# Four graph layers on one core: layer 0's transpositions moved to the ends of its rounds, layer 2's to a spare bank, sigmoid's table loaded early

## The chip, the core and the metric

The kernel runs on one core of a Trainium2 chip. A core has five engines with an instruction order each: PE (TensorE, matrix products into PSUM), ACT (ScalarE), DVE (VectorE), POOL (GpSimd) and SP, which here only starts transfers. They run beside each other and meet at semaphores; each takes its own instructions strictly in order, so an instruction that waits holds up all behind it. The metric is the time of one execution in device microseconds, as the median of several runs.

## The reference

The inputs are `x` (4096 nodes by 64 features), a dense 4096 x 4096 matrix `adj` of zeros and ones with a density of about 0.001, and small weights. Four layers follow each other, each as `x = x + layer(relu(layernorm(x)), adj)`:

```python
# layer 0: attention between all nodes, masked by adj
h = lorentz_linear(x, W, b, scale)           # a linear map; column 0 becomes sigmoid(.)*exp(scale)+1.1,
q = lorentz_linear(h, Wq, bq, scale_q)       # the other 63 are scaled to fit it
k = lorentz_linear(h, Wk, bk, scale_k)
att = sigmoid((2 + 2 * (qm @ k.T)) / att_scale + att_bias)    # qm: q with column 0 negated
support = (adj * att) @ h
out = support / sqrt(clip(abs(support[:, :1]**2 - sum(support[:, 1:]**2)), 1e-8))
# layer 1: out = w @ (input @ weight) + bias; w halves with each further neighbour from the last, 100 of them
# layer 2: out = 1 - 0.1 * x - 0.01 * sum(x * (adj @ x), axis=1)
# layer 3: out = relu(concat([X, (adj @ X) / max(deg, 1)]) @ W.T)
```

## The kernel before

**Tiling.** The nodes are cut into 8 blocks of 512 (`ib`, the receiving nodes) and into 32 tiles of 128 (the sending nodes), taken in pairs (`g`). `adj` comes transposed, a pair of tiles by a block at a time. POOL loads each such piece into SBUF as an 8-bit mask (`load_masks`, L175; 128 pieces). SP loads all of `adj` once more in f32 in the background, and DVE checks that it holds zeros and ones only (`check`, L356; `ck` in layer 0, `ckw` later). If it does not, a general version of the model runs after this one (`model(True)`); it is in the program but not executed with these inputs.

**Prologue.** `first_rows_and_block` lists the rows' preparation (`before0`: norm, h, q and k) and the first block's work with a cost and an earliest time for each step. A planner (`Listing.plan` and `run`) tries many orders against these costs and writes the best one out; PE's idle stretches are filled with products that nobody reads (`fill`, L1039). The step `bias_rows` on POOL has a planned cost too. ACT needs tables for its functions: the `Exp` of L104 loads one set, and the first `Sigmoid` (L664) makes it load another.

**Layer 0.** After the prologue the order is written by hand. The loop over `todo` goes through rounds of `sizes` tiles: four in a steady block, with `first = [4, 4, 3, 3]` at the beginning. For each tile of a round `scores` (L920) makes 128 x 1024 products on PE into a PSUM tile `ps`, for which there are three places (two in `pp`, one in `spare`); `sigmoids` (L933) runs on ACT, and `masked` (L944) multiplies with the mask on DVE into an SBUF tile `att`. In a round of four, the first tile's sigmoid goes straight into `att`, so that ACT already releases its `ps`; the others' sigmoids stay in `ps` until DVE has multiplied them. After a round's scores PE makes the sums (`gather`, L951) of the round before. After each tile the loop calls `load_masks(1)`, at some tiles `check()`, and `on()`, which takes one step of the small jobs.

**Jobs.** A job is a generator: what it issues up to its next `yield` goes into the engines' orders at that point. `rows0` handles a finished block of layer 0. It lets two steps pass, turns the sums with four transpositions on PE (`turned`, L231, tile `pt`, in the bank `pr` of the pool `pm`), has ACT copy them out (`halves_added`, L237), adds halves on POOL (`sup`, L239), squares on ACT (L892), and reduces on DVE (the group `inn`, L895 to L898). A reciprocal root in twelve small POOL instructions follows (`rsqrt`, L260 to L263), and `x_sb` is updated on POOL (L900, L901). Then `norm` starts the next layer: `st` on DVE (L271, L272), `xc` on POOL (L275), a square on ACT (L278), the group `va` on DVE (L281, L291, L256), the root on POOL, and `xc` again on DVE (L297). `split` makes two f16 numbers of each feature in `s2a`: the first on POOL (L245), the second on DVE (L248) two steps later. `queries` prepares the next block's queries: it waits six steps, makes two transpositions (`pq`, L859, also in `pr`) and has ACT copy them into `qt` in four pieces (L869).

**Layers 1 to 3.** Layer 1 counts neighbours on PE (`many`, L1168; `cnt`, L1235 and L1245), turns the counts into weights on ACT and DVE (`w`) and sums (L1273). Layers 2 and 3 sum with masks as one operand (`product`, L1345); every fourth product takes a step of the jobs (`beat`). `rows2` evacuates a block's sums, turns them in bank 3 (`turned`, L231), and later uses the banks 3 and 4 again: `ph` (bank 4, L1410) for transpositions, and `pn` (banks 3 and 4, L1422) for the products with layer 3's weights, which ACT copies into `fa` and `v` (L1430, L1431). The bank `pr` of `pm` is used in layer 1 by `rows1` and has no user in layer 2.

Of the kernel before, what the change touches and what calls it, by code (L numbers as in the profile page):

```python
# [11 lines left out]
F32 = mybir.dt.float32  # L12
# [4 lines left out]
AF = mybir.ActivationFunctionType  # L17
# [7 lines left out]
P = 128  # L25
# [23 lines left out]
def kernel(  # L49
# [12 lines left out]
    nc = tc.nc  # L62

    cpool = ctx.enter_context(tc.tile_pool(name="const", bufs=1))
# [37 lines left out]
    part = cpool.tile([P, QUAD], BF16, name="part")  # L102
    exp_s = cpool.tile([P, 3], F32, name="exp_s")
    nc.scalar.activation(exp_s, scal[:, 0:3], AF.Exp)  # L104

    att_a = cpool.tile([P, 1], F32, name="att_a")
    att_c = cpool.tile([P, 1], F32, name="att_c")
# [26 lines left out]
    def model(general):  # L134
# [15 lines left out]
        def rows_in(gr):  # L150
# [10 lines left out]
        todo = [  # L161
            (ib, g) for ib in order0 for g in (first_cols if ib == order0[0] else range(NG))
        ]
# [21 lines left out]
        s2a = parts.tile([P, NT, 2, D], FP16, name="s2a" + sfx)  # L185
# [53 lines left out]
            nc.gpsimd.tensor_tensor(to, v[:, :, 0:D], v[:, :, D:P], ALU.add)  # L239
            yield  # L240

        def split(h, s2, rows):


            nc.gpsimd.tensor_scalar(s2[:, rows, 0, :], h, 1.0 / STEP, None, ALU.mult)  # L245
            yield
            yield
            nc.vector.scalar_tensor_tensor(  # L248
                s2[:, rows, 1, :], s2[:, rows, 0, :], -STEP, h, ALU.mult, ALU.add
            )  # L250
# [599 lines left out]

        stream0 = pool("stream0", 1, l0) if general else None
        spare, turn = [], [0]
        qts = {}

        def queries_turned(ib, pt):
# [16 lines left out]
            qts[ib] = qt  # L872

        def queries(ib):
            for _ in range(6):
                yield
            pt = pm.tile([P, CI, P], F32, tag="pr", name=f"pq_{ib}{sfx}")
            queries_turned(ib, pt)
            yield
            queries_laid(ib, pt)  # L880

        def rows0(ib, asb):
            tag = f"0_{ib}"
            rows = block(ib)
            yield
            yield
            pt = turned(asb, None, tag)
            yield
            sup = rows_tile("sup", tag)
            yield from halves_added(sup, asb, pt)  # L890
            sq = rows_tile("sq", tag)
            nc.scalar.activation(sq, sup, AF.Square)  # L892
            yield
            inn = small("inn", tag)
            nc.vector.tensor_reduce(inn, sq, AX.X, ALU.add)  # L895
            nc.vector.scalar_tensor_tensor(inn, sq[:, :, 0], -2.0, inn, ALU.mult, ALU.add)
            nc.vector.scalar_tensor_tensor(inn, inn, -1.0, inn, ALU.mult, ALU.max)
            nc.vector.tensor_scalar(inn, inn, 1e-8, None, ALU.max)  # L898
            rs = rsqrt(inn, tag)
            nc.gpsimd.tensor_tensor(sup, sup, bc(rs, CI), ALU.mult)  # L900
            nc.gpsimd.tensor_tensor(x_sb[:, rows, :], x_sb[:, rows, :], sup, ALU.add)  # L901
            yield
            yield
            yield
            yield
            h = yield from norm(rows, None, tag, False)
            yield from split(h, s2a, rows)
            ready.setdefault(1, set()).add(ib)

            nc.gpsimd.tensor_tensor(  # L910
                x_sb[:, rows, :], x_sb[:, rows, :], over_rows(bias1, CI), ALU.add
            )
# [43 lines left out]
        def first_rows_and_block():  # L956


            listing = Listing()
            add = listing.add  # L960
            bias = add("POOL", 3.8, lambda _: bias_rows(), at=6.5)
            for n in range(0 if general else len(todo) * EARLY // NIB * 5 // 8):
                add("POOL", 0.56, lambda _: load_masks(1), at=2.2 * max(n - 5, 0))
            made = [before0(listing, gr, bias) for gr in range(len(ROWS))]
            v = SimpleNamespace(att=[], pt={}, acc=None, at=0)
            asked = {}
            last = NIB - 1

            def turn_q(ib):
                def emit(part):  # L970
                    v.pt[ib] = turn_tile(part, f"pq_{ib}")
                    queries_turned(ib, v.pt[ib])
                return emit

            for ib in (last, last - 1):
                hw, fq, ktd = made[0]
                q = add(
                    "PE", 0.45, turn_q(ib), fq[max(fq)], *asked.values(), takes=TURN
                )
                asked[ib] = add(  # L980
                    "ACT", 1.5, lambda _, ib=ib: queries_laid(ib, v.pt[ib]), q, frees=q
                )

            def make_room(_):
                v.acc = pa0.tile([P, IB], F32, tag="pa", name=f"acc0_{last}{sfx}")

            room = add("PE", 0.0, make_room, asked[last], takes=("pa",))
            slots = tuple(f"att{n}" for n in range(ATTS))
            scored, spread = [], []
            for n, (ib, g) in enumerate(todo[: NG + 2]):  # L990
                gr = next(i for i, (r0, m) in enumerate(ROWS) if r0 <= g * CG < r0 + m)
                hw, fq, ktd = made[gr]
                u = (g * CG - ROWS[gr][0]) // HR
                tile = SimpleNamespace(ib=ib, g=g)
                begun = n >= NG

                def emit_scores(_, tile=tile):
                    tile.ps = scores(tile.ib, tile.g)

                def emit_sigmoids(_, tile=tile):  # L1000
                    tile.att = sigmoids(tile.ps, att_tile(tile.ib, tile.g))

                def emit_masked(_, tile=tile):
                    masked(tile.ib, tile.g, tile.att, tile.att)
                    if tile.ib != last:
                        v.att.append((tile.ib, tile.g, tile.att))

                def emit_gather(_, tile=tile):
                    gather(v.acc, fb, tile.g, tile.att, v.at)
                    v.at += 1  # L1010

                sc = add(
                    "PE", 0.88, emit_scores, ktd[u], asked[ib], *(scored if begun else ()),
                    takes=("pp0", "pp1"), form="scores",
                )
                sg = add(
                    "ACT", 1.2, emit_sigmoids, sc, *(spread if begun else ()), frees=sc,
                    takes=slots,
                )
                mu = add("DVE", 1.25, emit_masked, sg)  # L1020
                if begun:
                    continue
                scored.append(sc)
                spread.append(sg)
                add("PE", 0.88, emit_gather, mu, hw[u], room, frees=sg, form="gather")


            v.idle = pp.tile([P, CG, IB], F32, tag="pp", name="idle" + sfx)
            v.filling = 0

            def fill(part):
                if part.engine != "PE" or v.filling is None:
                    return
                if part.form == "scores":
                    v.filling = None
                    return
                for _ in range(int((part.idle - 0.1) / 0.215) if v.filling else 50):
                    v.filling += 1
                    nc.tensor.matmul(  # L1039
                        v.idle[:, v.filling % CG, :], ones,  # L1040
                        ones.unsqueeze(1).to_broadcast([P, IB // P, P]),
                        start=True, stop=True, skip_group_check=True,
                    )
                v.filling = max(v.filling, 1)

            listing.run(("pm", "pa", "ps", "pp0", "pp1", *slots), fill)
            return v.acc, v.att

        with tc.manual_schedule():
# [20 lines left out]
            k, done = NG + 2, NG  # L1070
            for size in sizes:
                now = []
                for ib, g in todo[k : k + size]:
                    ps = scores(ib, g)

                    if size == 4 and not now:
                        att = frm = sigmoids(ps, att_tile(ib, g))
                    else:
                        frm, att = sigmoids(ps), att_tile(ib, g)
                    masked(ib, g, frm, att)  # L1080
                    now.append((ib, g, att))
                    load_masks(1)
                    k += 1
                    if k > 2 * NG and k % 8 in (0, 2, 4, 5, 7):
                        check()
                    on()
                for ib, g, att in late:
                    at = done % NG
# [6 lines left out]
                        push(rows0(ib, evacuated(ib, acc, 0)), 10)  # L1095
                    done += 1
                late = now
            if len(checks) % 2:
                check()
            if general:  # L1100
# [284 lines left out]
        def rows2(ib, acc):  # L1385
            tag = f"2_{ib}"
# [2 lines left out]
            asb = evacuated(ib, acc, 2, sums_level, third=ib % 3 == 2)  # L1389
            yield  # L1390
            yield
            pt = turned(asb, 3, tag)
            yield
            prod = rows_tile("prod", tag, epi2)
            yield from halves_added(prod, asb, pt)
# [197 lines left out]
```

## Time and profile before

| | |
|---|---|
| median of the runs | 599.48 us (599.21 to 599.6, 3 runs) |
| the profiled execution's own time | 599.52 us |
| its span | 597.7 us |
| granted TensorE clock, mean | 0.997 |
| busy share of the span | PE 97%, DVE 81%, ACT 56%, POOL 40% |
| prologue | 0 to about 47 us |
| layer 0 | to about 299 us |
| layer 1 | to about 461 us |
| layer 2 | to about 528 us |
| layer 3 | to the end |

The span runs from the first to the last event of the profiled execution; its own time has 1.8 us around the span. A row such as `L944 DVE TENSOR_TENSOR att<-ps,mask` names the line of the kernel, the engine, the operation, and what it writes and reads. `PEld` is PE's weight load, which overlaps with the products. "Idle before" and the name behind it say how long the engine stood still ahead of an instruction, and what ended that. In the timeline, instructions of the same kind that follow each other are one row (`x4`), with the start of the first and the time until the end of the last; f32 products appear as two instructions each, so a tile of scores is x4.

### The profile page before, as it was taken

How to read it: one execution, taken by the hardware profiler on the slowest of the kernel's cores; microseconds unless marked ns; L12 is line 12 of the kernel's file. 1: busy time of each engine (PE TensorE's matmuls, PEld its weight loads, DVE VectorE, ACT ScalarE, POOL GpSimd, SP SyncE). 2: the span in 40 equal slices, each digit the busy share in tenths (PEclk: the TensorE clock that was granted, in tenths of full speed). 3: DMA queues.
4: the chain of work that ended last, by engine and by line, in shares of the span. 5: the costliest groups of instructions: out<-in, count | busy, mean ns of one | idle time of the engine just before them, and what ended most of it. 6: DMA issues, size and time to landing. Idle time of an engine off the chain costs nothing.

```text
span 597.7 us, 9243 instructions
## 1 busy us (share of the span) xinstructions
PE 579.2 (97%) x3135; PEld 237.4 (40%) x3135; DVE 484.2 (81%) x941; ACT 335.7 (56%) x541; POOL 238.5 (40%) x459
## 2 busy tenths in 40 slices
PE   8899999899999999899999999999998999899995
PEld 3563333233333333233343343343443544454553
DVE  5878677699999997999966878979887769987753
ACT  1568665767676765666527677767765014431221
POOL 7534204456767676744344401001010315462252
PEclk9999999999999999999999999999999999999998
DMA  9995902799999998973182545546556476546921
GB/s 140 145 105 43 105 10 20 77 141 148 161 153 162 148 154 154 133 149 98 43 316 73 177 155 193 164 158 192 163 177 200 152 253 205 169 148 193 322 85 42
DMA packets 43016, 87.04 MB, mean 146 GB/s; under 512 B 5136, under 2 KB 22032, under 8 KB 42960
## 3 DMA queue, kind: packets, MB, share of 16 engines
q1 hardware_dynamic: 23808, 68.40, 34.9%
q0 software_dynamic: 18720, 17.57, 31.6%
q10 hardware_dynamic: 432, 0.40, 0.3%
q8 instruction: 26, 0.43, 0.3%
q14 instruction: 30, 0.25, 0.1%
HBM read 135.63 MB, written 1.05 MB: 229 GB/s over the span
## 4 chain that ended last, share of the span: by engine, by line
PE 86%; DVE 5%; ACT 3%; issue 2%; POOL 2%; DMA 2%; ACTq 0%; DVEq 0%; POOLq 0%
PE acc L1345 19%; PE ps L920 17%; PE acc L951 17%; PE acc L1273 10%; PE cnt L1235 9%; PE cnt L1245 3%; PE many L1168 2%; PE pt L231 2%; PE idle L1039 2%; DVE att L944 1%; PE pr L1148 1%; DMA vec<-vecs_dram 1%; PE pn L1422 1%; ACT qt L869 1%; PE ps_q L628 1%
## 5 line engine op out<-in xcount | busy, mean ns | idle before, releaser
L356 DVE SCALAR_TENSOR_TENSOR ckw<-ckw 128x1024 f32<-128x1024 f32 x98 | 124.8, 1281 | 5.6 <-DMA ckw<-adjt_dram 5.3
L920 PE MATMUL ps<-qt,kt 64*128 64x512 f32 x512 | 125.2, 613 | 3.7 <-DVE att L944 3.4
L951 PE MATMUL acc<-att,fb 128*64 128x512 f32 x512 | 118.3, 600 | 0.0
L1261 ACT ACTIVATE w<-cnt 128x512 int16<-128x512 f32 x176 | 93.1, 597 | 42.8 <-PE cnt L1245 42.3
L944 DVE TENSOR_TENSOR att<-ps,mask 128x1024 f32<-128x1024 f32 x84 | 101.1, 1219 | 9.8 <-ACT ps L933 8.9
L933 ACT ACTIVATE ps<-ps,att_c,att_a 128x1024 f32<-128x1024 f32 x84 | 95.7, 1173 | 10.0 <-PE ps L920 6.9
L933 ACT ACTIVATE att<-ps,att_c,att_a 128x1024 f32<-128x1024 f32 x44 | 52.2, 1203 | 53.4 <-PE ps L920 52.8
L175 POOL DMA_DIRECT2D mask<-adjt_dram x128 | 70.2, 560 | 19.7 <-DMA mask<-adjt_dram 17.5
L920 PEld LDWEIGHTS ps<-qt,kt 64*128 64x128 f32 x512 | 44.1, 185 | 74.7 <-DVE att L944 21.4
L1259 DVE TENSOR_SCALAR w<-cnt 128x512 int16<-128x512 f32 x80 | 53.6, 686 | 22.9 <-PE cnt L1245 22.4
L944 DVE TENSOR_TENSOR att<-att,mask 128x1024 f32<-128x1024 f32 x44 | 56.0, 1288 | 17.2 <-ACT att L933 16.8
L1235 PE MATMUL cnt<-mask,after 128*128 128x512 fp8e4 x256 | 66.3, 379 | 2.1 <-DVE w L1259 1.6
L1273 PE MATMUL acc<-w,s2a 128*128 128x512 bf16 x256 | 66.5, 382 | 0.1
L951 PEld LDWEIGHTS acc<-att,fb 128*64 128x64 f32 x512 | 33.3, 136 | 79.4 <-issue 71.4
L275 POOL TENSOR_TENSOR xc<-x_sb,st 128x256 f32<-128x256 f32 x24 | 19.1, 794 | 108.5 <-DVE st L272 55.0
L1345 PE MATMUL acc<-mask,s2a 128*128 128x512 fp8e4 x256 | 57.8, 379 | 0.0
L1345 PE MATMUL acc<-mask,s2b 128*128 128x512 fp8e4 x256 | 57.7, 379 | 0.0
L260 POOL TENSOR_TENSOR rs_a<-rs_y 128x4 f32<-128x4 f32 x48 | 16.8, 351 | 81.4 <-DVE rs_y L256 72.2
L356 DVE SCALAR_TENSOR_TENSOR ck<-ck 128x512 f32<-128x512 f32 x60 | 44.9, 748 | 0.2 <-DMA ck<-adjt_dram 0.2
L1235 PEld LDWEIGHTS <-after 128*128 128x128 bf16 x256 | 24.8, 99 | 31.0 <-issue 3.4
L1345 PEld LDWEIGHTS <-s2b 128*128 128x128 f16 x256 | 25.0, 98 | 27.5 <-issue 0.8
L1345 PEld LDWEIGHTS <-s2a 128*128 128x128 f16 x256 | 24.6, 98 | 27.3
(196 smaller groups left out, 604.1 us busy)
## 6 DMA issues: line engine op xcount, KB each, us to landing
ckw<-adjt_dram SPq DMA_DIRECT2D x98, 512.0 KB, 3.4
mask<-adjt_dram POOLq DMA_DIRECT2D x128, 128.0 KB, 9.0
ck<-adjt_dram SPq DMA_DIRECT2D x60, 256.0 KB, 5.4
x_sb<-x_dram SPq DMA_DIRECT2D x4, 256.0 KB, 8.0
out_dram<-y POOLq DMA_DIRECT2D x6, 128.0 KB, 2.2
out_dram<-y ACTq DMA_DIRECT2D x2, 128.0 KB, 2.1
w_sb<-wts_dram SPq DMA_DIRECT2D x2, 80.0 KB, 7.7
vec<-vecs_dram ACTq DMA_DIRECT2D x1, 130.5 KB, 6.5
```

The lines of the kernel that those rows point to most:

```text
L175: nc.gpsimd.dma_start(out=masks[ib][:, g * CG : (g + 1) * CG, :], in_=adjt[ib, g])
L275: nc.gpsimd.tensor_tensor(xc, xr, bc(st, CI), ALU.add)
L356: nc.vector.scalar_tensor_tensor(at, at, 0.0, at, ALU.not_equal, ALU.not_equal, accum_out=odd[:, k : k + 1])
L920: nc.tensor.matmul(ps[:, c, :], kt[half, g, :], qts[ib][half, :], start=True, stop=True)
L933: nc.scalar.activation(to, ps, AF.Sigmoid, bias=att_c, scale=att_a)
L944: nc.vector.tensor_tensor(att, frm, mask, ALU.mult)
L951: nc.tensor.matmul(acc[c * D : (c + 1) * D, :], lhs[:, t, :], rhs[:, c, :], start=(at == 0), stop=(at == NG - 1), skip_group_check=True,)
L1235: nc.tensor.matmul(cnt, after, masks[ib][:, t, :], start=True, stop=True, skip_group_check=True)
L1259: nc.vector.tensor_scalar(w, cnt, 0.0, None, ALU.max)
L1261: nc.scalar.activation(w, cnt, AF.Relu)
L1273: nc.tensor.matmul(accs[ib], both(s2a, t), w, start=(t == NT - 1), stop=False, skip_group_check=True,)
L1345: nc.tensor.matmul(acc, both(s2, t), masks[ib][:, t, :], start=(t == 0), stop=(t == NT - 1), skip_group_check=True,)
```

## The change

- `exp_s` is followed by a sigmoid of one column into a tile that nobody reads (`tried`), so ACT loads sigmoid's table there.
- In layer 0's loop a flag `edge` is true only at a round's last tile, and for good after the loop. `rows0` waits one step and then for the flag, instead of two steps. `queries` waits three steps and then for the flag, instead of six.
- Rounds of three tiles, too, send the first tile's sigmoid to `att`.
- `split` waits four steps instead of two for the features 0 and 1.
- `rows2` turns its sums in the bank `pr` instead of bank 3.
- The planner's cost for `bias_rows` is 8.1 instead of 3.8.

```diff
     exp_s = cpool.tile([P, 3], F32, name="exp_s")
     nc.scalar.activation(exp_s, scal[:, 0:3], AF.Exp)
 
+    tried = cpool.tile([P, 1], F32, name="tried")
+    nc.scalar.activation(tried, exp_s[:, 0:1], AF.Sigmoid)
...
-        def split(h, s2, rows):
+        def split(h, s2, rows, steps=2):
 
             nc.gpsimd.tensor_scalar(s2[:, rows, 0, :], h, 1.0 / STEP, None, ALU.mult)
-            yield
-            yield
+            for _ in range(steps):
+                yield
...
         spare, turn = [], [0]
+
+        edge = [False]
         qts = {}
...
         def queries(ib):
-            for _ in range(6):
+            for _ in range(3):
+                yield
+            while not edge[0]:
                 yield
             pt = pm.tile([P, CI, P], F32, tag="pr", name=f"pq_{ib}{sfx}")
...
             rows = block(ib)
             yield
-            yield
+            while not edge[0]:
+                yield
             pt = turned(asb, None, tag)
...
-            yield from split(h, s2a, rows)
+            yield from split(h, s2a, rows, 4 if ib < 2 else 2)
...
-            bias = add("POOL", 3.8, lambda _: bias_rows(), at=6.5)
+            bias = add("POOL", 8.1, lambda _: bias_rows(), at=6.5)
...
-                for ib, g in todo[k : k + size]:
+                for n, (ib, g) in enumerate(todo[k : k + size]):
+                    edge[0] = n == size - 1
                     ps = scores(ib, g)
 
-                    if size == 4 and not now:
+                    if size > 2 and not now:
                         att = frm = sigmoids(ps, att_tile(ib, g))
...
                 late = now
+            edge[0] = True
...
-            pt = turned(asb, 3, tag)
+            pt = turned(asb, None, tag)
```

## The prediction

> **What bounds the kernel now.** I read the page's busy times first, then busy time by stretch for one block of layer 0, then who waited for whom on PE, then the timelines of those places.
>
> ```profile
> PE 579.2 (97%) x3135; PEld 237.4 (40%) x3135; DVE 484.2 (81%) x941; ACT 335.7 (56%) x541; POOL 238.5 (40%) x459
> ...
> 141.71:171.94 30.23, 30.23 (x137) 10.38 (x135) 28.44 (x49) 21.14 (x24) 20.83 (x47) 1.00 1.02 157
> ...
> PE ps L920 <- DVE att L944: 3.4, 4, 1.6
> PE pt L231 <- ACT v L1431: 2.1, 4, 0.5
> ```
>
> PE sets the end: it has almost no gaps, and its clock is full (PEclk 9 throughout). But the second line (one block of layer 0: length, PE, PEld, DVE, ACT, POOL busy) shows DVE busy 28.44 of 30.23 us, so a PE that gets faster soon meets DVE. PE's own waits are few: 3.4 us for mask products in layer 0, 2.1 us in layer 2.
>
> PE in one steady block (columns: start, length, then the instruction):
>
> ```profile
> 126.70 3.70 PE L920 MATMUL ps<-qt,kt 64*128 64x512 f32 x16
> 130.34 3.65 PE L951 MATMUL acc<-att,fb 128*64 128x512 f32 x16
> 133.92 2.85 PE L920 MATMUL ps<-qt,kt 64*128 64x512 f32 x12
> 136.70 0.44 PE L859 MATMUL pq<-ident,s2a 128*128 128x128 f32 x2
> 137.06 1.13 PE L920 MATMUL ps<-qt,kt 64*128 64x512 f32 x4
> 138.12 3.65 PE L951 MATMUL acc<-att,fb 128*64 128x512 f32 x16
> 141.71 3.70 PE L920 MATMUL ps<-qt,kt 64*128 64x512 f32 x16
> ```
>
> Start to start, four tiles' scores take 3.64 unbroken, but 2.78 + 1.06 = 3.84 when a transposition cuts them: a cut costs 0.20 besides the transposition (pq 0.36; pt 0.59, at 151.70). I call a block's four rounds A, B, C, D: 7.22 us each (3.64 scores + 3.58 sums), with pt in B and pq in D before.
>
> The other engines around the start of an A (141.71):
>
> ```profile
> 139.47 1.53 ACT L869 COPY qt<-pq 64x256 f32<-64x256 f32 x4
> 140.78 2.73 POOL L175 DMA_DIRECT2D mask<-adjt_dram  x5
> 143.48 0.68 POOL L275 TENSOR_TENSOR xc<-x_sb,st 128x256 f32<-128x256 f32 x1
> 144.19 0.42 ACT L278 ACTIVATE sq<-xc 128x256 f32<-128x256 f32 x1
> 144.51 3.35 ACT L933 ACTIVATE ps<-ps,att_c,att_a 128x1024 f32<-128x1024 f32 x3
> 145.70 1.22 DVE L944 TENSOR_TENSOR att<-ps,mask 128x1024 f32<-128x1024 f32 x1 [0.33 <-ACT ps L933]
> ```
>
> The four qt copies lie where ACT has nothing else. xc is ready just as ACT comes to its square, and DVE already waits 0.33. There is room for three tiles of scores in PSUM, and only a round's first tile is released by ACT; so a round's third scores wait for the last mask product of the round before. In A that product ended at 150.57, and PE needed its place at 148.93 + 1.71 = 150.64: 0.07 of slack.
>
> **The change part by part.** Sums are against the profiled execution: span 597.7 and 1.8 around it, 599.52; the median shown is 599.48.
>
> *Sigmoid's table.*
>
> ```profile
> 21.93 0.58 ACT L650 COPY t<-ps_h 128x512 f32<-128x512 f32 x1 [1.21 <-PE ps_h L628]
> 22.54 1.28 ACT L664 ACT_TABLE_LOAD   x1
> 23.83 0.23 ACT L664 ACTIVATE sgh<-t 128x16 f32<-128x16 f32 x1
> ```
>
> The load costs 1.28 here and moves behind exp_s (ends 7.51), where ACT idles until 10.07: loaded by about 8.8, and the one-column sigmoid adds about 0.2. What follows does not gain 1.28: DVE is busy with xc until 24.11 and took up rrh at 24.61, so that way gains 0.5; ACT's next copy (25.01) needs a transposition done at about 24.7, so the second half of the rows gains 0.3. I take -0.3, between 0 and -0.5. The Trainium skill (ScalarE: Activation LUTs, What ACT_TABLE_LOAD costs) puts a switch at about 2.66, with a drain of 1.38 behind the load. No such drain shows between 23.82 and 23.83. With it the early load would end at 10.17, 0.1 late, and the later gain is capped by the same 0.3 to 0.5; I go by the row.
>
> *bias_rows' planned cost, 8.1 for 3.8.* The instruction order built from the changed kernel keeps every engine's prologue, its PE fillers too, except one 0.2 us DVE instruction (fold) two places earlier in the same unbroken run: 0. Queues of SP: no transfer moves. POOL's mask loads keep their numbers between the row steps in the steady blocks.
>
> *Start of layer 0, to 126.70.*
>
> ```profile
> 109.92 1.99 PE L920 MATMUL ps<-qt,kt 64*128 64x512 f32 x8
> 113.48 1.99 PE L920 MATMUL ps<-qt,kt 64*128 64x512 f32 x8 [1.57 <-DVE att L944]
> 115.40 2.80 PE L951 MATMUL acc<-att,fb 128*64 128x512 f32 x12
> 118.12 1.99 PE L920 MATMUL ps<-qt,kt 64*128 64x512 f32 x8
> 120.41 1.13 PE L920 MATMUL ps<-qt,kt 64*128 64x512 f32 x4 [0.30 <-DVE att L944]
> 121.47 0.66 PE L231 MATMUL pt<-ident,asb 128*128 128x128 f32 x4
> ```
>
> The first round here took 5.48 for 3.64. Now the two rounds of three also let ACT release their first tile, and the qt copies (at 106.70, ahead of three sigmoids) go a round earlier. Followed through: scores of this round start at 109.7; of the tiles whose places they need, the first is free at 106.6, the second at 109.6, the third only after the 1.6 us of constants on DVE, at about 112.3, against a need at 111.4. So about 0.9 of the 1.84 stays: -0.9. One cut less ahead of it: -0.2. In the next round the wait of 0.30, which broke the run (0.2), and the cut (0.2): -0.7. I take the sum, -1.8, between -0.9 and -2.2. C and D of that block lose one cut: -0.2.
>
> *The steady blocks (features 4 to 1).* Each loses two cuts: -0.40. Against it stand two moves that the instruction order shows. First, qt now stands on ACT in D behind the first sigmoid: that runs from 1.20 to 2.33 of D, the copies take 1.5, the next sigmoid starts at 3.83, its mask product at 5.03 (4.2 without the copies), then product, check (0.61), product (products 1.14 apart), the last from 7.92 to 9.20; A's third scores want its place at 7.22 + 1.71 = 8.93: PE waits 0.27. Second, the rows' inn group comes one product and one check later, and C also has s2a and the copy of pt ahead of it: from C's start 2.42 + four products at 1.14, two checks at 0.61, s2a 0.34 and 0.23 of waiting give 8.77, for 6.44 before (133.14 less 126.70). C and D last 7.58 + 7.22 = 14.80, so inn starts 6.03 ahead of A, for 8.57. From inn to xc on POOL took 143.48 less 133.14 = 10.34, so xc starts 4.31 after A, its square is over at 5.3, and as the square is queued ahead of the third sigmoid, that comes at 5.33; mask product 6.54 to 7.68, va group 0.76, last product to about 9.7. B starts at 7.49 and wants that place at 9.20: PE waits 0.50. Per block +0.27 + 0.50 - 0.40 = +0.37; for four blocks +1.5. If both waits vanished it were -1.6; the upper end is the last rival's.
>
> That chain on POOL holds twelve small instructions, 0.2 each alone (97.78 to 101.15, 3.37 in all), but 4.91 from 134.50 to 139.41, where one of them took 1.08 beside DVE's product with both operands in SBUF. The Trainium skill (SBUF — State Buffer, Who interferes with whom) says such a DVE instruction and a GpSimd one that reads SBUF block each other, the later for the whole of the earlier. This speaks against the change, which leans on that chain: with two checks (0.69) and such a product (1.23) in it, it would be 3.4 + 2.6 = 6.0, the wait 1.6, and the four blocks +5.9. The row, with the same three beside it, says 4.9; I keep it.
>
> *The last block* has no mask loads between x_sb and xc (all 128 are issued by its start), so only qt's 0.27 is left against 0.40: -0.1. split's two more steps for features 0 and 1: s2a is wanted in layer 1 some 4 us after its new place: 0; if that cover goes, DVE waits once for POOL, about 1.
>
> *The pause of 2.1 us on POOL at 232.24* (released by nothing shown), which made that block 32.5 for 30.5: its place in POOL's order stays, so kept; -2 if it does not come again.
>
> *Layer 2's sums in the spare bank.*
>
> ```profile
> 502.39 0.71 PE L1422 MATMUL pn<-wxn_sb,ht 64*128 64x128 f32 x8
> 503.62 0.66 PE L231 MATMUL pt<-ident,asb 128*128 128x128 f32 x4 [0.52 <-ACT v L1431]
> 504.11 2.75 PE L1345 MATMUL acc<-mask,s2b 128*128 128x512 fp8e4 x12
> ```
>
> Four waits of 0.52 for v to leave bank 3 go: 2.1. The other bank was emptied a block ago. DVE needs about 6.1 of a block's 6.36 (rs at 504.50, 510.56), PE would take 5.8, so DVE falls back 0.3 a block; sup is done 1.5 ahead of its transposition, enough for the four. I take -2.0, down to -1.2 if DVE's lag reaches PE.
>
> Sum: -0.3 - 1.8 - 0.2 + 1.5 - 0.1 - 2.0 = -2.9, from 599.5 to 596.6.
>
> **The rivals.** *The cuts are won in full:* the row chain is hidden, as POOL's small instructions alone would make it (3.4), and the four blocks give -1.6: sum -6.0, 593.5. For it: DVE has 1.8 us a block free. Against: DVE's order, not its load, makes the waits. *Only traded:* constants keep the early stall (-0.9), DVE caps layer 2 (-1.2), the blocks pay +0.6 each: -0.3 - 0.9 - 0.2 + 2.4 - 0.1 - 1.2 = -0.3, 599.2. *Slower:* the POOL chain ahead of xc is lengthened as the skill's rule has it; each block pays 1.5: the four +6.0, sum +1.6, 601.1. The other parts give -4.4, so it decides from (4.4 + 1.2)/4 = 1.4 a block.
>
> **How the numbers follow.** Chances: forecast 0.46 (its own range 595.2 to 598.3), cuts in full 0.22, traded 0.18, slower 0.14. What this kernel's measurement can tell from no change is about 0.2%, 1.2 us: 598.3 to 600.7. Faster: 0.44 + 0.22 + 0.03 = 0.69; slower 0.14; same 0.17. The range runs from just below the second case to between the two last, 593.2 to 600.6, leaving out about 0.07 below and 0.10 above.
>
> **What would show it.** Right: no table load after 20 us; the round near 110 about 4.5 long; in each steady block waits of PE's scores for DVE's products, together 0.5 to 1 us, with ACT's square waiting for xc before the third sigmoid; blocks of 30.5 to 31; no wait of pt for v, and 2 us less in layer 2. Wrong: blocks under 30 (second case), POOL's chain over 6 us (slower), or PE waiting on sup in layer 2.

## The result and the profile after

The changed kernel takes 596.21 us, the one before 599.40 in the runs beside it: a ratio of 0.9949, 95% interval 0.9936 to 0.9962. The forecast was 596.6. The total came out close, but partly by luck: two terms that the forecast had at nothing, -1.9 and +1.6, are each nearly as large as its largest gain, and most of them cancels. The rest of this text is mostly about these two.

The profiled execution took 596.21, for 599.52 before. By stage, from the starts of PE's groups in the two traces:

| stage | before | after | difference | forecast |
|---|---|---|---|---|
| to the first scores of layer 0's loop (84.18, 83.91) | 84.18 | 83.91 | -0.27 | -0.3 |
| from there to C of feature 5 (126.70, 124.51) | 42.52 | 40.60 | -1.92 | -1.8 |
| C and D of feature 5 | 15.01 | 14.80 | -0.21 | -0.2 |
| four steady blocks | 123.84 | 123.18 | -0.66 | +1.5 |
| last block, to its last scores | 22.44 | 22.74 | +0.30 | -0.1 |
| last scores to layer 2's first product | 173.12 | 174.76 | +1.64 | 0 |
| layer 2 | 67.34 | 65.16 | -2.18 | -2.0 |
| layer 3 | 63.86 | 63.91 | +0.05 | 0 |
| sum | | | -3.25 | -2.9 |

Some executions of nearly every kernel, the one before too, are about 1.6 us longer, and the medians hold both kinds, so stages are compared within profiled executions; the profiled one of layer 2's bank alone (599.09) is a long one, with a granted clock of 0.86 and 0.80 in its stretches 25 to 30 and 30 to 35 us and everything behind these 1.6 later.

The page's busy times, one steady block by stretch (length, then busy times of PE, PEld, DVE, ACT, POOL), and PE's waits, after the change:

```profile
PE 577.4 (97%) x3135; PEld 238.2 (40%) x3135; DVE 482.1 (81%) x941; ACT 335.4 (56%) x542; POOL 241.7 (41%) x459
...
169.67:200.60 30.93, 30.32 (x136) 10.52 (x135) 28.23 (x49) 21.08 (x24) 21.22 (x47) 1.00 1.02 157
...
PE ps L928 <- DVE att L952: 2.5, 4, 0.6
...
PE pw L1196 <- ACT asb L212: 1.7, 1, 1.7
```

PE is busy 1.8 us less: the same 512 score products take 122.9 us for 125.2, as fewer of their runs are broken by a transposition or a wait. The wait of pt for v is gone from the list; the wait for mask products is shorter in total, but it has changed its kind: before, two of its four were single events of 1.6 and 1.4 us, now all four are about 0.6, one in the round at 109.4 and one in each of the last three steady blocks. And pw, the first product of layer 1, waits 1.7 for ACT where it waited 0.7.

The first of the new kind, in B of a steady block (rows picked from the timeline: start, length, then the instruction):

```profile
169.67 3.92 PE L928 MATMUL ps<-qt,kt 64*128 64x512 f32 x16
...
174.32 0.66 POOL L278 TENSOR_TENSOR xc<-x_sb,st 128x256 f32<-128x256 f32 x1
175.01 0.42 ACT L281 ACTIVATE sq<-xc 128x256 f32<-128x256 f32 x1 [1.87 <-POOL xc L278]
175.34 2.26 ACT L941 ACTIVATE ps<-ps,att_c,att_a 128x1024 f32<-128x1024 f32 x2
176.53 1.23 DVE L952 TENSOR_TENSOR att<-ps,mask 128x1024 f32<-128x1024 f32 x1 [0.89 <-ACT ps L941]
177.10 1.99 PE L928 MATMUL ps<-qt,kt 64*128 64x512 f32 x8
179.71 1.99 PE L928 MATMUL ps<-qt,kt 64*128 64x512 f32 x8 [0.61 <-DVE att L952]
181.62 0.66 PE L234 MATMUL pt<-ident,asb 128*128 128x128 f32 x4
```

Read it downward: A's scores start at 169.67, xc starts 4.65 later, the square waits for it 1.87, the third sigmoid waits behind the square, and DVE waits 0.89 for that sigmoid. Its product ends at 177.7, the sums of va (0.76) and the round's last product follow, and that ends at 179.66; PE has stood since 179.1 without the place that it frees. B takes 8.70 us. Unbroken scores, the transposition and the sums are 3.64 + 0.59 + 3.58 = 7.81. So the wait of 0.61 costs 0.89: it also breaks the run of scores, as a cut did. A, 7.43 for 7.22, loses its 0.2 inside the run of the first line: 3.92 us for the 3.70 of an unbroken one, with no wait that the list shows.

### The profile page after: what moved, and what is told of

Same layout as the page of the kernel before. It is cut to its first block, busy times and chain, and to the rows that moved or that the text cites. A ratio compares the mean times of both kernels' runs of the same rounds, so it can differ in the third digit from the quotient of the medians.

```text
span 594.4 us, 9236 instructions
## 1 busy us (share of the span) xinstructions
PE 577.4 (97%) x3135; PEld 238.2 (40%) x3135; DVE 482.1 (81%) x941; ACT 335.4 (56%) x542; POOL 241.7 (41%) x459
## 3 DMA queue, kind: packets, MB, share of 16 engines
q0 software_dynamic: 18720, 17.57, 31.6%
## 4 chain that ended last, share of the span: by engine, by line
PE 78%; DVE 7%; POOL 5%; DMA 4%; ACT 2%; issue 2%; SPq 0%; POOLq 0%; DVEq 0%; ACTq 0%
PE acc L1355 19%; PE ps L928 15%; PE acc L959 15%; PE acc L1283 9%; PE cnt L1245 8%; PE cnt L1255 3%; DVE att L952 2%; PE idle L1047 2%; PE pt L234 2%; DMA ckw<-adjt_dram 2%; PE pr L1158 1%; POOL rs_a L263 1%; DMA vec<-vecs_dram 1%; DMA mask<-adjt_dram 1%; PE pn L1432 1%
## 5 line engine op out<-in xcount | busy, mean ns | idle before, releaser
L928 PE MATMUL ps<-qt,kt 64*128 64x512 f32 x512 | 122.9, 609 | 2.8 <-DVE att L952 2.5
L952 DVE TENSOR_TENSOR att<-ps,mask 128x1024 f32<-128x1024 f32 x82 | 98.4, 1216 | 8.4 <-ACT ps L941 8.3
L941 ACT ACTIVATE ps<-ps,att_c,att_a 128x1024 f32<-128x1024 f32 x82 | 93.4, 1176 | 1.5 <-PE ps L928 1.4
L941 ACT ACTIVATE att<-ps,att_c,att_a 128x1024 f32<-128x1024 f32 x46 | 54.6, 1203 | 58.3 <-PE ps L928 57.8
L263 POOL TENSOR_TENSOR rs_a<-rs_y 128x4 f32<-128x4 f32 x48 | 18.2, 378 | 69.8 <-DVE rs_y L259 67.2
L359 DVE SCALAR_TENSOR_TENSOR ck<-ck 128x512 f32<-128x512 f32 x60 | 43.1, 718 | 0.2 <-DVE att L952 0.2
```

Of the source, the lines that this page charges most:

```text
L263: nc.gpsimd.tensor_tensor(a, y, y, ALU.mult)
L359: nc.vector.scalar_tensor_tensor(at, at, 0.0, at, ALU.not_equal, ALU.not_equal, accum_out=odd[:, k : k + 1])
L928: nc.tensor.matmul(ps[:, c, :], kt[half, g, :], qts[ib][half, :], start=True, stop=True)
L941: nc.scalar.activation(to, ps, AF.Sigmoid, bias=att_c, scale=att_a)
L952: nc.vector.tensor_tensor(att, frm, mask, ALU.mult)
```

## The experiments

**Layer 2's bank alone** (on the kernel before).

```
-            pt = turned(asb, 3, tag)
+            pt = turned(asb, None, tag)
```

> The kernel before with one edit of the change: layer 2's turned sums go to the spare bank instead of bank 3. Theory (the four waits of 0.52 for v are the whole of it, and DVE does not take over as the bound inside layer 2): 2.1 to 2.2 us less, 597.2 to 597.4, no wait of pt for v, a layer-2 block of about 5.8 us in place of 6.36. Rival (DVE's 6.1 us of work a block caps it): 1.2 us less, 598.2, with PE waiting on sup at the later transpositions.

Measured: 597.53 us, ratio 0.9958 (0.9943 to 0.9973). From layer 2's first product to layer 3's takes 65.16 us, as in the changed kernel, for 67.34; no wait of pt is left. The theory holds: 2.18 for four waits of 0.52, and DVE doesn't cap it.

**The table alone** (on the kernel before).

```
     nc.scalar.activation(exp_s, scal[:, 0:3], AF.Exp)
+    tried = cpool.tile([P, 1], F32, name="tried")
+    nc.scalar.activation(tried, exp_s[:, 0:1], AF.Sigmoid)
```

> The kernel before with one edit: the sigmoid of one column right behind the exponentials, so that its table is loaded at about 7.5 us. Theory: 0.1 to 0.3 us less (599.1 to 599.4), as the profile of the changed kernel starts its loop 0.27 earlier, 0.13 of which is an earlier arrival of the constants. Rival (the drain of 1.38 that the Trainium skill adds to a switch is real and is saved too): 1 us or more less, 598.5 or under.

Measured: 599.38 us, ratio 0.9993 (0.9985 to 1.0001), which is no difference that this measurement tells from none. Its profiled execution starts the loop at 83.94, for 84.18 before, but part of this is that the constants arrive earlier: from the start of exp_s to the loop it takes 76.72 us (from 7.22) for 76.87 (from 7.31). That is 0.15, at the lower end of the theory. The timeline of ACT in the changed kernel shows what the load costs:

```profile
7.40 1.28 ACT L107 ACT_TABLE_LOAD   x1
8.70 0.20 ACT L107 ACTIVATE tried<-exp_s 128x1 f32<-128x1 f32 x1
9.95 1.23 ACT L547 ACTIVATE sq<-xc 128x512 f32<-128x512 f32 x2 [1.04 <-DVE xc L542]
```

The next instruction starts 0.02 after the load, and the load itself 0.02 after exp_s (7.18, 0.20 long). The Trainium skill (ScalarE: Activation LUTs, What ACT_TABLE_LOAD costs) adds a drain of 1.38 to a load's 1.28 and doesn't say on which side; behind the load it would have put the next instruction at 10.06. Neither side shows it here. The row decides: 1.28, all of it hidden, since ACT idles another 1.04 before sq.

**The changed kernel without layer 0's moves**: rows turned after two steps, queries after six, s2a split after two; the table, the condition on rounds of three and the bank stay.

```
-            for _ in range(3):
-                yield
-            while not edge[0]:
+            for _ in range(6):
                 yield
...
-            while not edge[0]:
-                yield
+            yield
...
-            yield from split(h, s2a, rows, 4 if ib < 2 else 2)
+            yield from split(h, s2a, rows, 2)
```

> The changed kernel with the transpositions of layer 0 back at their old steps (rows after two steps, queries after six, split after two); table, rounds of three and bank stay. Theory (the moves cost more than the cuts they save: in each of four steady blocks 0.22 of waiting in A and 0.61 in B against 0.40 of cuts, 1.0 at the end of layer 0, 0.3 to 0.4 in layer 1; they save 0.2 and 0.4 at the start): 596.2 - 1.7 - 1.0 - 0.4 + 0.6 = 593.7, if POOL's pause of 2 us does not come; 595.7 if it comes. Rival (the saved cuts are what the moves are worth, 0.40 a block): 598 or more.

Measured: 598.48 us, ratio 0.9975 (0.9961 to 0.9988), the profiled execution 597.30. The median would be the rival's, but between the profiled executions the moves are worth 1.1 (597.30 less 596.21), which is neither the theory's loss nor the rival's 0.40 a block: both missed. The stage table of this run shows why: from the loop's start to C of feature 5 it takes 42.50 us, the time of before to 0.02, and PE's wait in the first round is back in full (timeline of PE):

```profile
113.29 1.99 PE L925 MATMUL ps<-qt,kt 64*128 64x512 f32 x8 [1.56 <-DVE att L949]
```

So the condition on rounds of three, which stayed, is worth nothing by itself; all of the start's 1.9 belongs to the moves. And the block at 232.89 takes 32.50 us, as before: the pause of POOL is back with the rows' old place. The loop to C of feature 5 gives 1.9 of the moves' worth and the four blocks 0.7; layer 1 and the last block take 1.8 back.

**The changed kernel without the condition on rounds of three.**

```
-                    if size > 2 and not now:
+                    if size == 4 and not now:
```

> The changed kernel without the condition on rounds of three: only rounds of four give their first tile back to PSUM through ACT. Theory (the early stall shrank because of the condition and the earlier copies of the queries together, neither alone): the wait at 112 is back at 1.5 and the round at 109.4 at 5.4 or more, 597.1. Rival (the earlier copies alone did it, as the condition alone changed nothing): 596.2, the wait at 0.63.

Measured: 596.08 us, ratio 0.9949 (0.9935 to 0.9962), the wait at 111.9 is 0.60. The rival holds: with the moves in place the condition changes nothing. That it is the copies of the queries, and not the rows, which shortened the stall, the run with the rows back below shows: its wait there is 0.20. In the changed kernel the round that took 5.48 takes 4.54, and the next one runs unbroken:

```profile
112.06 1.99 PE L928 MATMUL ps<-qt,kt 64*128 64x512 f32 x8 [0.63 <-DVE att L952]
...
116.70 3.71 PE L928 MATMUL ps<-qt,kt 64*128 64x512 f32 x16
```

**One mask load more at the loop's first tile** (on the kernel before).

```
-                    load_masks(1)
+                    load_masks(2 if k == NG + 2 else 1)
```

> The kernel before with one mask load more at the loop's first tile (two in place of one), so that every later load is one place earlier in POOL's order; nothing else moves. Theory (the pause of 2.08 us belongs to the 114th mask load: it stood there in every profile so far, on the way to xc in the kernel before and in POOL's idle time in the changed kernel): the pause moves to about 221, where POOL has nothing to do, the block of 32.5 comes down to 30.6, and the time to 597.4. Rival (the pause belongs to the place behind x_sb, or to the time): it stays at 232 and the time at 599.4.

Measured: 596.95 us, ratio 0.9965 (0.9954 to 0.9977). The theory holds, and this is the run that explains most. Counted from the first, in all 14 profiles kept, the load in front of which POOL stands still with no releaser is the 114th of 128, wherever it is issued (mask loads on POOL; the first line is of the kernel before, where the row is a batch that starts with the 114th):

```profile
234.32 2.73 POOL L175 DMA_DIRECT2D mask<-adjt_dram  x5 [2.08 <-issue]
```

The changed kernel:

```profile
222.91 0.54 POOL L178 DMA_DIRECT2D mask<-adjt_dram  x1 [1.41 <-issue]
```

The kernel before with one load more:

```profile
221.53 0.54 POOL L175 DMA_DIRECT2D mask<-adjt_dram  x1 [0.77 <-issue]
```

Before, this load stood behind x_sb and ahead of xc, with all of the row chain behind it. In the other two it comes a batch earlier, when POOL has nothing else to do until 227.16 in the changed kernel and 225.48 in this one; the idle time of 1.41 or 0.77 is hidden, and the next batch (231.86 here) starts without any. The block comes down from 32.48 to 30.57; the rest of the 2.5 is 0.3 in the second steady block, 0.2 in layer 1 and 0.15 ahead of the loop, where the constants arrive earlier. What POOL waits for there no view shows, and no run varied it. A load moves 144 packets (18720 of its queue less 288 for the outputs, over 128 loads), so the pause comes when 113 loads have asked for 16272; a limit on that count would fit and is untested.

**The rows' transposition back alone** (on the changed kernel; queries stay at the end of a round).

```
-            while not edge[0]:
-                yield
+            yield
...
-            yield from split(h, s2a, rows, 4 if ib < 2 else 2)
+            yield from split(h, s2a, rows, 2)
```

> The changed kernel with the rows' transposition back after two steps (and split after two), the queries' still at the end of a round. Theory (the wait of 0.61 in B and the 1.0 at the end of layer 0 come from the row chain being late): B unbroken at 3.64 plus one cut, A still waits 0.2 behind the copies of the queries; 596.2 - 4 x 0.4 - 1.0 - 0.3 + 0.2 = 593.5. Rival (DVE's load makes the waits, wherever the rows are turned): the wait stays at 0.6 a block and the cut comes on top, 597 or more.

Measured: 597.49 us, ratio 0.9954 (0.994 to 0.9967): four over the theory's time and in the rival's range. B has no wait (8.01 with its cut), as the theory says and the rival does not, and the end of layer 0 and layer 1 together take 173.07, as before. But A now takes 8.01, with a wait of 0.52 and a broken run (7.43 in the changed kernel), so the block is 30.82; and with the rows the pause came back (32.44 for the fourth block). The wait in A (timeline of DVE and PE):

```profile
171.53 0.42 DVE L274 TENSOR_REDUCE st<-x_sb 128x4 f32<-128x256 f32 x1
171.98 0.17 DVE L275 TENSOR_SCALAR st<-st 128x4 f32<-128x4 f32 x1
...
172.09 1.22 DVE L951 TENSOR_TENSOR att<-ps,mask 128x1024 f32<-128x1024 f32 x1
...
173.37 1.99 PE L927 MATMUL ps<-qt,kt 64*128 64x512 f32 x8 [0.52 <-DVE att L951]
```

So the mechanism in B and at the layer's end holds. The expectation left out the pause, and took A's wait for the copies' alone: with the rows early DVE's st stands ahead of D's last mask product, as it did before the change (141.31), and the copies' delay comes on top of it.

**The copies of the queries later** (on the changed kernel, behind D's fourth sigmoid).

```
             queries_turned(ib, pt)
-            yield
+            for _ in range(4):
+                yield
             queries_laid(ib, pt)
```

> The changed kernel with one move: the four copies into qt stand behind D's fourth sigmoid, where ACT is idle, while the transposition pq stays at the end of C. Theory (A waits because the copies stand behind D's first sigmoid and delay the mask products): A goes from 7.43 back to 7.22 in four blocks and the last one, 1.1 less than 596.2, 595.1. Rival (DVE's load sets the wait, wherever the copies stand): the wait of A stays or B's grows by as much, 596.2.

Measured: 598.36 us, ratio 0.997 (0.9956 to 0.9985): 2 us over the changed kernel. A is unbroken at 7.22, so what it lost was indeed the copies'. But B grows from 8.70 to 9.31 (its PE timeline):

```profile
179.15 1.13 PE L929 MATMUL ps<-qt,kt 64*128 64x512 f32 x4 [0.20 <-DVE att L953]
...
181.05 1.99 PE L929 MATMUL ps<-qt,kt 64*128 64x512 f32 x8 [0.77 <-DVE att L953]
```

Here xc starts 5.05 after A, for 4.65: x_sb's addition on POOL took 1.22 for 0.72, beside a check on DVE (171.74 to 172.42), and DVE's st waits 0.61 for it. And PE comes to B 0.2 earlier, so it waits twice there. The first round of the loop also lost its gain (wait 1.56), as its queries too are copied late.

**The square later** (on the changed kernel; features 6 to 1; for feature 1 the steps behind the square root's rows are two instead of three).

```
-            yield
+            for _ in range(2 if tag[:2] == "0_" and tag != "0_0" else 1):
+                yield
             sq = rows_tile("sq", tag)
             nc.scalar.activation(sq, xc, AF.Square)
```

> The changed kernel with ACT's square of the rows one step later, behind the third sigmoid of A, in features 6 to 1 (for feature 1 the step is taken out again behind the square root's rows). Theory (B waits because the square waits for xc ahead of the third sigmoid; the wait of 0.61 costs 0.88, since it also breaks the run of scores): B goes from 8.70 to about 7.8 in three blocks, 2.7 less, 593.5; the wait at the end of layer 0 stays. Rival (the wait moves to the next thing that is late: the fourth sigmoid, or DVE's sum va behind the square): under 1 us less, 595.2 or more.

Measured: 595.73 us, ratio 0.9928 (0.9907 to 0.9948): the time is in the rival's range. B is at 7.81, as the theory says, but a wait appears in A:

```profile
172.00 1.99 PE L928 MATMUL ps<-qt,kt 64*128 64x512 f32 x8 [0.37 <-DVE att L952]
```

A went from 7.43 to 7.86, so the block is 30.47 for 30.93: half the gain goes into A. That the copies are what delays DVE there is read from the runs below, in which the copies are late too and A is unbroken.

**Feature 1's square behind the copy of the last sums** (on the changed kernel). On the changed kernel's timeline, the end of layer 0 is this:

```profile
295.23 0.42 DVE L274 TENSOR_REDUCE st<-x_sb 128x4 f32<-128x256 f32 x1 [0.61 <-POOL x_sb L909]
...
296.73 0.42 ACT L281 ACTIVATE sq<-xc 128x256 f32<-128x256 f32 x1 [5.86 <-POOL xc L278]
297.05 0.57 ACT L212 COPY asb<-acc 128x512 f32<-128x512 f32 x1
297.67 0.43 PE L1196 MATMUL pw<-wn_size,one 64*128 64x64 f32 x2 [1.72 <-ACT asb L212]
```

PE's sums end at 295.95; ACT has been idle for 5.86, but its next instruction in order is the square, which waits for POOL. The copy stands behind it.

```
-            yield
+            for _ in range(3 if tag == "0_1" else 1):
+                yield
             sq = rows_tile("sq", tag)
```

(and one step instead of three behind the square root's rows for this feature).

> The changed kernel with feature 1's square two steps later, so that on ACT it stands behind the copy of the last sums instead of ahead of it. Theory (the 1.72 at the start of layer 1, for 0.69 before, is that copy waiting behind the square, and the square for the late chain of rows): pw comes 1.0 earlier, 595.2; 594.9 if the 0.3 at 319 goes too. Rival (the wait moves on into the counting of layer 1, which needs feature 1's rows or the same engines): 596.2.

Measured: 596.61 us, ratio 0.9952 (0.9934 to 0.9971). pw comes at 296.73, 1.0 earlier in the stage, exactly as expected, and waits 0.69. But from the last scores to layer 2 it still takes 174.96, for 174.76. PE waits in layer 1 instead (waits of 0.81 and 1.01 for w):

```profile
314.42 0.59 PE L1245 MATMUL cnt<-mask,after 128*128 128x512 fp8e4 x2 [0.81 <-DVE w L1269]
```

DVE is late there because xc, which waits for POOL, and inn of the rows stand ahead of w; at 320.01 (1.01) it is st of the next rows, which waits 2.05 for POOL's x_sb. The rival holds: the late rows are paid for somewhere, and the copy was only the first place.

**The three moves together** (late copies, late square, feature 1's square behind the copy).

> The changed kernel with the three moves of the runs beside it together: copies of the queries behind D's fourth sigmoid, the square behind A's third, feature 1's square behind the copy of the last sums. Theory (three waits, each with its own cause, so that they add up): 596.2 - 1.1 - 2.7 - 1.0 = 591.4. Rival (DVE is near its limit, 28.4 of 30.2 us a block, and gives back a wait for each that is taken away): 594 or more, with DVE's idle time in a block under 0.5.

Measured: 593.44 us, ratio 0.9893 (0.987 to 0.9916). In the steady blocks the theory holds in full: no waits, A 7.22, B 7.81, C 7.58, D 7.22, block 29.83. The square has moved out of the way of the sigmoid that DVE needs (timeline of ACT and PE):

```profile
202.29 2.26 ACT L942 ACTIVATE ps<-ps,att_c,att_a 128x1024 f32<-128x1024 f32 x2
...
205.74 0.42 ACT L282 ACTIVATE sq<-xc 128x256 f32<-128x256 f32 x1 [1.18 <-POOL xc L278]
...
207.20 3.70 PE L929 MATMUL ps<-qt,kt 64*128 64x512 f32 x16
```

xc is even later here (5.06 after A), and no engine waits for it in a way that reaches PE. DVE is busy 28.30 of the 29.82 us, idle 1.5: not the limit that the rival made it, and the time is under the rival's 594. What is missing from 591.4 is the start (wait 1.69 at 113, late copies) and layer 1 (from the last scores to layer 2 175.02).

**The same with the start's copies early**: those of feature 5 stand where the changed kernel has them, and feature 1's rows too (the square is late for the features 6 to 2 only).

```
-            for _ in range(4):
+            for _ in range(1 if ib == 5 else 4):
```

> The changed kernel with the copies of the queries behind the fourth sigmoid, except the first ones of the loop, which stay a round early, and the square behind the third sigmoid for features 6 to 2; feature 1 as in the changed kernel. Theory: steady blocks of 29.83 with no wait, as with the three moves, and the start of the changed kernel (the wait at 112 at 0.6 in place of 1.69, the round after it unbroken): 1.0 under the three moves, 592.3. Rival (the start needs the late copies' other order too): 593.3.

Measured: 591.85 us, ratio 0.9874 (0.9859 to 0.989). The theory holds: the start takes 40.61, as in the changed kernel (wait 0.64), the blocks 29.83.

**And feature 1's rows turned in the middle of a round again.**

```
+            if ib == 1:
+                yield
-            while not edge[0]:
+            while ib != 1 and not edge[0]:
                 yield
...
-            yield from split(h, s2a, rows, 4 if ib < 2 else 2)
+            yield from split(h, s2a, rows, 2 if ib else 4)
```

> The same, and feature 1's rows turned at their old place, in the middle of a round (and split after two steps). Theory (late rows of feature 1 cost 1.5 to 2 from the last scores to layer 2, 174.8 against 173.1, whether as a wait for the last sums' copy or as waits in layer 1; early rows cost one cut of 0.2): 1.5 under the kernel beside it, 590.8. Rival (layer 1 pays for something else): 592.3 or more.

Measured: 591.44 us, ratio 0.987 (0.9855 to 0.9885), the lowest median of all, but only 0.4 under the run beside it, whose executions overlap with these (591.59 to 592.12, and 591.18 to 591.67). In the profiled executions, from the last scores to layer 2 takes 174.08, for 175.03 in the run beside it and 173.12 in the kernel before: 0.95 of the 1.9 to be had, and B of the last block pays 0.2 for its cut. What is left is two waits:

```profile
283.11 1.99 PE L932 MATMUL ps<-qt,kt 64*128 64x512 f32 x8 [0.21 <-DVE att L956]
...
313.31 0.42 DVE L274 TENSOR_REDUCE st<-x_sb 128x4 f32<-128x256 f32 x1 [1.42 <-POOL x_sb L913]
...
314.63 0.59 PE L1249 MATMUL cnt<-mask,after 128*128 128x512 fp8e4 x2 [0.43 <-DVE w L1273]
```

The second is the known kind: feature 0's rows are still late in this kernel, and their st, which waits 1.42 for POOL, stands ahead of w on DVE. The first breaks the last round's run, which takes 4.11 for 3.64; why DVE is later there than before the change isn't settled.

## Why the prediction was right or wrong

*Right, term by term.* C and D of feature 5: 0.21 against 0.2. Layer 2: 2.18 against 2.0; the 0.1 held back for DVE's lag wasn't needed. `bias_rows` at nothing: from exp_s to the loop it takes 76.73 us in the changed kernel and 76.72 in the table alone, which lacks that edit.

*Right in its number by luck: the table.* The stage lost 0.27 for 0.3, but exp_s itself started 0.13 earlier, as the constants arrived earlier. Counted from exp_s the table is worth 0.14; the run with one load more, which lacks it, takes 76.88, as the kernel before takes 76.87. The cap was read rightly, its size not: ACT's next copy (25.01 before) starts at 24.72, where it waits for PE's transposition, and 0.13 of these 0.29 are the earlier constants.

*The steady blocks: the mechanism and its sum.* The forecast was +0.37 a block from two waits and the cuts. Without the pause the four blocks grew by 1.25 (before's own first three, 30.57 for the fourth) or by 1.55 (against the run with one load more): +0.31 to +0.39. The chain was followed rightly: from inn to xc took 10.35 us (10.34 forecast), xc started 4.65 after A (4.31) and the third sigmoid 5.67 (5.33). The sizes inside were off and made up for each other. A loses 0.22 (0.27 forecast). B's wait is 0.61 (0.50; none in the first of the four), but costs 0.89, because a wait of PE in a run of scores breaks it as a cut does. And the cuts saved 0.74 a block in the later ones, not 0.40: before, a block was 30.57 = 4 x 7.22 + 0.87 + 0.82, after, transpositions cost only 0.59 and 0.36. The order of ACT was read right: square ahead of the third sigmoid, and its move alone took B's wait away.

*The rule on shared ports: it holds, and the sum made from it was wrong.* In the changed kernel (timeline of DVE and POOL):

```profile
165.09 1.22 DVE L952 TENSOR_TENSOR att<-att,mask 128x1024 f32<-128x1024 f32 x1
165.33 1.04 POOL L263 TENSOR_TENSOR rs_a<-rs_y 128x4 f32<-128x4 f32 x1 [5.13 <-DVE rs_y L259]
...
166.23 0.68 DVE L359 SCALAR_TENSOR_TENSOR ck<-ck 128x512 f32<-128x512 f32 x1
...
166.45 0.52 POOL L264 TENSOR_TENSOR rs_a<-rs_a,inn 128x4 f32<-128x4 f32 x1
...
167.06 0.19 POOL L265 TENSOR_SCALAR rs_a<-rs_a 128x4 f32<-128x4 f32 x1
```

Both lengthened instructions end 0.06 after the DVE instruction beside them. So it is in layer 0 of the kernel before, without exception: the 35 small instructions that start while DVE runs a mask product or a check with both operands in SBUF end 0.05 to 0.06 after it, and the 121 others take about 0.2, also beside products with an operand in PSUM. That is the block of which the Trainium skill speaks (SBUF — State Buffer, Who interferes with whom). But an instruction that comes late to it waits only for what is left of the other, so the rule gives 3.37 + 0.84 + 0.32 = 4.53 here, where the chain took 4.51 (165.33 to 169.84), and about 4.9 in the row of before, which took 4.91. The 6.0 of the forecast charged the whole length of all three. The second check now meets the step behind the chain (sup, 1.03 for 0.61). The forecast did well to keep the row, and the slower rival never came near 1.4 a block.

*The failed step: "its place in POOL's order stays, so kept".* The row chain is issued one step later; each step issues a mask load; so one more load stands ahead of the chain, and the 114th is no longer the one ahead of xc. The pause fell into POOL's idle time: -1.9. The forecast named this gain ("-2 if it does not come again") and took the wrong side. One added load in the kernel before takes 2.5 us off by itself, three quarters of what the whole change brings.

*The failed step: "s2a is wanted in layer 1 some 4 us after its new place: 0", and with it the last block's -0.1.* The later rows of feature 1 reach the end of layer 0. There ACT's square waits for POOL ahead of the copy that starts layer 1, and in layer 1 DVE's st waits for POOL ahead of w: +1.64 up to layer 2, 1.03 as pw's wait and 0.6 in layer 1, 0.3 of it as a wait for w. I followed s2a, the chain's result, and not the chain's other instructions through the queues of ACT and DVE to the stage's end. In the last block A still loses 0.22 and B 0.27, and the forecast's 0.40 of saved cuts was 0.2, since no queries are turned there and B's cut is its only one: +0.30.

*A right number with a wrong half: the start.* -1.92 for -1.8, but the part that I gave to rounds of three letting ACT release their first tile is worth nothing. With the rows back at their old place the start takes 41.16, for 42.50 without any move and 40.60 with all: 1.3 is the earlier copies of the queries, 0.6 the rows' cut and the wait beside it.

The other terms stand within 0.3 of the traces each, like for like. The total came out because -1.9 and +1.6 + 0.4 fell on opposite sides: that is luck.

## What to carry to other kernels

When a step of a software pipeline moves, write out the order of every engine across the stage's end, and look for instructions that wait there ahead of work that is ready; the result's deadline is not enough. A wait that goes can make another one longer, since PE then comes early to the next place: two moves that gave -0.5 and +2 alone gave in the steady blocks all they promised, together. And a pause with no releaser on a queue is worth one run that shifts the count of what is issued: here a single number was worth 2.5 us.

## What the runs showed of the hardware

POOL pauses in front of its 114th mask load, in whichever place that stands: 2.07 to 2.08 us in the five profiles where the load follows other work at once, 0.25 to 1.41 of visible idle time in the nine where POOL comes to it early. Its cause is open.

A small POOL instruction that starts while DVE runs an instruction with both operands in SBUF ends 0.05 to 0.06 us after that one (35 of 35 in layer 0 of the kernel before).

A load of ACT's tables took 1.28 us, and the next activation that was ready started 0.01 to 0.02 us behind it.

A wait of 0.61 in a run of score products cost PE 0.89.
